# An fp32 cross-attention kernel on one core: product 6 of y by blocks from the second batch on, its state copied back into the bank, and two sums moved one period ahead

## The chip, the cores and the metric

The kernel runs on one core of a Trainium2 chip. Its time is device microseconds (us) of one execution; the median of 3 runs of the kernel before is 683.82 us (683.69 to 684.1). Beside these there is one profiled execution. The engines are called by their names in the profile: PE (TensorE, matmuls), PEld (its weight loads), DVE (VectorE), ACT (ScalarE), POOL (GpSimd) and SP (SyncE, which here only issues DMAs).

## The reference

Eight batches; x1 and x2 are 512 x 1024 each, all in fp32. Cut to what matters:

```python
q = einsum('bcn,dc->bnd', x1, Wq) + bq            # 1024 x 64
k = einsum('bcn,dc->bdn', x2, Wk) + bk            # 64 x 1024
v = einsum('bcn,dc->bdn', x2, Wv) + bv            # 512 x 1024
attn = softmax(einsum('bnd,bdm->bnm', q, k), axis=2)
out = einsum('bcm,bnm->bcn', v, attn) + x1
```

The kernel computes y = x2 times the unnormalised exponentials e, scales its columns by one over their sums, and then computes o = Wv y + bv + x1.

## The kernel before, in words

**Two products of matrices per batch, each in seven.** Both y and o are computed by the Winograd form of Strassen's method: with halves of rows, columns and depth, seven products (numbered 1 to 7, table MULT) of sums of quarters take the place of eight. For y the left operands are quarters of x2 transposed (`a["11"]` to `a["22"]`) and their sums S1 to S4, the right ones are quarters of e (`t["11"]` to `t["22"]`) and their sums T1 to T4. All operands lie in SBUF, [128, 4, 256] on the left and [128, 4, 512] on the right. The products accumulate in two pairs of PSUM banks, "a" and "c" (`a0`, `a1`, `c0`, `c1`), each bank [128, 512]: product 1 opens bank a, products 6 and 5 are added to it, so that after each of the three the bank holds a state (P1, P1+P6, P1+P6+P5) that some result needs. The states are taken out to SBUF as `s.tmp[1]`, `[6]` and `[5]`. The other four PSUM banks are two slots with the tag "sc".

**Plain and blocked products.** A plain product (`multiply`, line 374, matmuls at line 389) takes 8 matmuls of 512 columns (16 records in the trace, since an fp32 matmul shows as two). A blocked one uses the same seven-product scheme once more inside: 7 inner products (`inner_product`, line 452, matmuls at line 456) of 2 matmuls of 256 columns each, 28 records. Its order is fixed as inner products 1, 7, 6, 2, 5, 4, 3 and its operands are sums which DVE makes beforehand: `inner_left` (line 421) gives four steps of 256 columns in the order S3, S1, S2, S4, and `inner_right` (line 433) three steps, T1 and T3 in one of 1024 columns, then T2 and T4 of 512 each. Inner product 7 needs inner S3 and T3, inner product 6 needs inner S2 and T2, inner product 3 needs inner S4. `multiply_seeded` (line 473) starts from empty banks; inner results that have more than one destination go through an "sc" slot and an ACT copy. `multiply_onto` (line 503) adds to a bank that already holds something: what can go straight to the bank does, the rest is copied by ACT into an SBUF tile d; then `complete` (a DVE addition on d) and `join` (two DVE additions of bank and d, one for each row block) give the sum. The bank alone is then not the state.

**A period.** `period` (line 780) writes out one batch's order by hand; tc.manual_schedule keeps each engine to the order of the program. In batches 1 to 7 PE runs: products 1 and 2 of y (blocked), 6 (plain, `first(6)`), the four score tiles of the next batch's first half and, except in the last two batches, the queries of the batch after that, then products 5, 7 and 3 (blocked), scores of the second half, keys, product 4 (blocked), and the seven plain products of o (`second`). Batch 6 has no queries and no keys in between, batch 7 no scores either. DVE meanwhile makes the operands of the blocked products, takes results out of PSUM, folds maxima and sums (`folds`, `fold_halves`, lines 249 to 253), and subtracts the maximum (line 302). POOL reduces over the partitions (`highest`, line 268, and `total`, line 272, both PARTITION_ALL_REDUCE) and issues the accumulating DMAs. `weave` interleaves several lists, one step of each in turn.

**Around the change.** At the start of a late period the program has, for DVE: T1 and T2 (`sum_e`, line 315, four additions of 1024 columns), `complete` of product 1, the sum of half 1 folded (with the four `inner_left` steps of product 7 woven in), a reciprocal, `complete` of product 2, `evict_y` of 11, then the operands of product 5 and S4 (line 109), then the maxima of the next batch's scores. Just in front of it, at the end of the period before, DVE has the operands of products 1 and 2 of the new batch, then `fold_halves` of the sum of half 0 (which waits for an accumulating DMA of POOL, `add_tile`, line 636), then the two additions of `evict_o` 21.

Of the kernel before, what the change touches and what calls it, by code (L numbers as in the profile page):

```python
# [16 lines left out]
def kernel(  # L17
# [294 lines left out]
    def right_sums(t, k):  # L312

        x, y = {"T1": ("12", "11"), "T2": ("T1", "22"), "T3": ("22", "12"), "T4": ("21", "T2")}[k]
        nc.vector.tensor_tensor(t[k], t[x], t[y], ALU.add if k == "T4" else ALU.subtract)
# [8 lines left out]
    def sum_t4(s):  # L324

        s.t["T4"] = t4 = sb.tile([P, MH, H], F32, tag="eT4", name=f"eT4_{s.b}")
        if s.b == 0:
            sum_e(s, "T4")
            return
        for i in (0, 2):  # L330
            nc.scalar.copy(t4[:, i : i + 2, :], s.t["21"][:, i : i + 2, :])
        for i in (0, 2):
            nc.gpsimd.dma_start(t4[:, i : i + 2, :], s.t["T2"][:, i : i + 2, :], accum_op=ALU.add)

    def sum_t3(s, i):

# [3 lines left out]

    def copy_u1(s, j):
        if j == 0:
            s.tmp[1] = sb.tile([P, 2, H], F32, tag="yT1", name=f"uy1_{s.b}")
        nc.scalar.copy(s.tmp[1][:, j, :], s.bank["a", j])

    def sum_e(s, *ks):
        parts = [{n: v[:, i : i + 2, :] for n, v in s.t.items()} for i in (0, 2)]
        for k in ks:
            for part in parts:
                right_sums(part, k)  # L350

    def sum_y(s, k):
        y = s.y
# [149 lines left out]
    def multiply_onto(s, i, d_tag, v_tag, hooks={}):  # L503

        bank = MULT[i][2]
        b0, b1 = (s.bank[bank, j] for j in range(2))  # L510
        chain, third = inner_parts(s, i)
        d = sb.tile([P, 2, 2, H // 2], F32, tag=d_tag, name=f"d{i}_{s.b}", bufs=1 + (d_tag == "a21"))
        v = sb.tile([P, 2, H], F32, tag=v_tag, name=f"v{i}_{s.b}")[:, 0, left]
        steps = {
            1: (chain, True, d[:, 0, 0, :]),
            7: (third, True, v),
            6: (chain, False, d[:, 1, 0, :]),
            2: (b0[:, left], False),
            5: (chain, False, d[:, 0, 1, :], d[:, 1, 1, :]),
            4: (b1[:, left], False),  # L520
            3: (b0[:, right], False),
        }
        for z in (1, 7, 6, 2, 5, 4, 3):
            inner_product(s, i, z, *steps[z])
            if z in hooks:
                hooks[z]()

        def complete():
            both = v.unsqueeze(1).to_broadcast([P, 2, H // 2])
            nc.vector.tensor_tensor(d[:, 1], d[:, 1], both, ALU.add)  # L530

        return d.rearrange("p j a n -> p j (a n)"), complete
# [3 lines left out]
        d, complete = multiply_onto(s, 4, "u5" if s.b < B - 1 else "a21", "r", hooks)  # L536
        return [complete, lambda: nc.vector.tensor_tensor(s.tmp[6], s.tmp[6], d, ALU.add)]

    def multiply_5(s, hooks):

        s.tmp[5], complete = multiply_onto(s, 5, "u5", "r", hooks)
        complete()

        def join(j):
            d = s.tmp[5][:, j, :]
            nc.vector.tensor_tensor(d, s.bank["a", j], d, ALU.add)

        return [lambda: join(0), lambda: join(1)]

    def copy_7(s, j):  # L550
        if j == 0:
# [219 lines left out]
    def scores_and(n, h, i_bank, bank, project):  # L771

        for i in range(MH):
            scores(n, h, i, bank if i == i_bank else None)()
        return project()
# [4 lines left out]
    def period(s, n, nn, nnn):  # L780
# [3 lines left out]
        def first(i):  # L784
            multiply(s, "y", i, s.a, s.t, MH)
# [18 lines left out]

        def scores_0(*rows):
            then = scores_and(n, 0, 1, "c", next_queries if nn else nothing)
            weave(folds(n, 0, "max", ALU.max), *rows)
            highest(n, 0)
            return then
# [6 lines left out]
            copy_first(n, 0)  # L816
            add_tile(n, 0, 1)

        open_t(s)
        if n is None:  # L820
            load_x(s, x1)
        if s.b == 0:
            first(1)
            head_second(s, n)
            sum_e(s, "T1", "T2")
            fold_halves(s, 0, ALU.add)
            total(s, 0)
            load_a(n, "11")
            first(2)
            evict_y(s, "11")  # L830
            keys(n)
            load_x(nn, x1)
            sum_t4(s)
            sums(s, 1)
            shares(s, 0)
            sum_e(s, "T3")
            load_a(n, "21", "22")
            first(6)
            scores_0()
            weave(inner_left(s, 4, s.a["22"], "a12"), inner_right(s, 4, s.t["T4"], "eT2"))  # L840
            lefts_3 = inner_left(s, 3, s.a["S4"], "aI3")
            shares(s, 1)
            first(5)
            weave(lefts_3, inner_right(s, 3, s.t["22"], "eT1"))
            for i in range(MH):
                lower(n, 0, i)
            first(7)
            copy_7(s, 0)
            copy_7(s, 1)
            complete_3 = multiply_seeded(s, 3, "r")  # L850
            complete_3()
            evict_t3(s)
            evict_y(s, "22")
            scale_y(s, "T3", "11", "22")
        else:
            complete_1 = multiply_seeded(s, 1, "y11")
            sum_e(s, "T1", "T2")
            complete_1()
            if n:
                weave(folds(s, 1, "sum", ALU.add), inner_left(s, 7, s.a["S3"], "yT4"))  # L860
            else:
                weave(inner_left(s, 5, s.a["S1"], "i2"), inner_right(s, 5, s.t["T1"], "y21", "u1"))
                weave(folds(s, 1, "sum", ALU.add), inner_left(s, 7, s.a["S3"], "yT4"))
            total(s, 1)
            invert(s, 0)
            complete_2 = multiply_seeded(
                s, 2, "y22", {5: lambda: copy_u1(s, 0), 4: lambda: copy_u1(s, 1)}
            )
            if n:
                sum_t3(s, 0)  # L870
                sum_t3(s, 2)
            complete_2()
            evict_y(s, "11")
            if n is None:
                sum_e(s, "T3")
            sum_t4(s)
            first(6)
            if n:
                weave(
                    inner_left(s, 5, s.a["S1"], "i2"),  # L880
                    inner_right(s, 5, s.t["T1"], "y21", "u1"),
                    [lambda: sum_a(s, "S4")],
                )
            else:
                sum_a(s, "S4")
            evict_q = None
            if n:
                evict_q = scores_0()
            spread(s, 0)
            shares(s, 1)  # L890
            weave(inner_right(s, 7, s.t["T3"], "yT1", "yT2"), inner_left(s, 3, s.a["S4"], "aI3"))
            join_5 = multiply_5(s, {6: evict_q} if nn else {})
            weave(join_5, inner_right(s, 3, s.t["22"], "eT1"))
            if n:
                lower(n, 0, 0)
            complete_7 = multiply_seeded(s, 7, "y12")
            complete_7()
            evict_y(s, "22")
            if n:
                for i in range(1, MH):  # L900
                    lower(n, 0, i)
            else:
                weave(inner_left(s, 4, s.a["22"], "a12"), inner_right(s, 4, s.t["T4"], "eT2"))

            hooks = {2: lambda: copy_7(s, 0), 5: lambda: copy_7(s, 1)}
            if n:
                hooks |= {6: lambda: exponential(n, 0, 0), 4: lambda: exponential(n, 0, 1)}
            complete_3 = multiply_seeded(s, 3, "r", hooks)
            complete_3()
            evict_t3(s)  # L910
# [17 lines left out]
        tops = folds(n, 1, "max", ALU.max) if n else []  # L928
        if s.b == 0:
            value_sums("S1", "S2")  # L930
        if late and n:
            tops.pop(0)()
        sum_y(s, "T1")
        if s.b == 0:
# [7 lines left out]
            if nn is None:  # L942
                hooks[7] = first_sum
        join_4 = multiply_4(s, hooks)
        weave(join_4, tops[:2] if late else [])
        if late and n:
            negate(n, "S3")
        if n:
# [3 lines left out]
        evict_y(s, "21")  # L952
        lefts_1 = rights_2 = []
        if late and n:
            tops[2]()
            lefts_1 = inner_left(n, 1, n.a["11"], "i2")
            rights_2 = inner_right(n, 2, n.e[0][:, 1], "eT4")
        scale_y(s, "21")
# [1 line left out]
            step()  # L960
        sum_y(s, "T4")
        if late and n:
            highest(n, 1)
            add_11(n, "S3")
            weave(rights_2, lefts_1[1:])
# [32 lines left out]
        if n:  # L998
            rows = [inner_right(n, 1, n.e[0][:, 0], "yT1", "yT2"), inner_left(n, 2, n.a["12"], "aS4")]
            if s.b == 0:  # L1000
                rows += [inner_right(n, 2, n.e[0][:, 1], "eT4")]
            weave(*rows)
            second(3)
            evict_o(s, "12")
            second(4)
            fold_halves(n, 0, ALU.add)
            total(n, 0)
            evict_o(s, "21")
        else:
            second(4)  # L1010
            evict_o(s, "21")
            second(3)
            evict_o(s, "12")
# [37 lines left out]
```

## Time and profile before

| what | us |
|---|---|
| median of the runs shown | 683.82 |
| the profiled execution, its own time | 684.41 |
| its span in the trace | 682.6 |
| PE busy in the span | 672.3 (98%) |
| DVE busy | 602.6 (88%) |
| ACT busy | 337.7 (49%) |
| POOL busy | 224.5 (33%) |
| period of batches 1 to 5 | about 82.0 each |
| period of batch 6 | 78.85 |
| batch 7 to the end of the span | 73.03 |

A period is counted from the first matmul of its product 1 to that of the next (120.58, 202.58, 284.57, 366.56, 448.60, 530.72 and 609.57 us from the start of the span). In the timeline each line gives the start, the length, the engine, the line of the kernel, the operation, what it writes and reads, the number of instructions merged into the line, and in brackets the idle time of the engine just before with what ended it. An instruction's length overlaps the next one's start by some 0.07 us, so what a chain of DVE instructions takes is read from start to start.

### The profile page before, as it was taken

To read this page: it belongs to the slowest core of one execution; us is meant where nothing else is said; L and a number is where in the kernel's file an instruction comes from. 1 tells how busy PE (TensorE), PEld (TensorE's weight loads), DVE (VectorE), ACT (ScalarE), POOL (GpSimd) and SP (SyncE) were. 2 spreads that over 40 slices of the span, in tenths; PEclk is the share of its full clock that TensorE was granted. 3 is DMA by queue.
4 is the path that set the end of the run, shared out by engine and by line. 5 is a ranking of instruction groups with operands and counts; after the bars stand their busy time and mean duration, and the time that the engine had idled before them with its cause. 6 is when DMAs were issued, how large, how long until landed. Compare 5 with 4: busy or idle time off the path is not lost.

```text
span 682.6 us, 7284 instructions
## 1 busy us (share of the span) xinstructions
PE 672.3 (98%) x2444; PEld 402.4 (59%) x2444; DVE 602.6 (88%) x783; ACT 337.7 (49%) x570; POOL 224.5 (33%) x182
## 2 busy tenths in 40 slices
PE   9999999999999999999999999999999999899997
PEld 5333554757546665557646485474854767457753
DVE  1999898799999799889999899988999979969984
ACT  2744266366454464553744647535565446454320
POOL 0124215260454313542144421445025440452300
PEclk9999999999999999999999999999999999999999
DMA  9655758968896939959499694996969873489503
GB/s 301 269 192 210 184 204 149 244 126 249 240 248 168 252 101 296 224 155 267 110 293 234 151 267 110 269 227 142 255 121 223 212 167 49 92 155 270 132 12 111
DMA packets 50772, 131.09 MB, mean 192 GB/s; under 512 B 5552, under 2 KB 7856, under 8 KB 50736
## 3 DMA queue, kind: packets, MB, share of 16 engines
q0 software_dynamic: 22464, 54.60, 44.1%
q1 hardware_dynamic: 27984, 75.64, 30.8%
q10 hardware_dynamic: 288, 0.39, 0.2%
q8 instruction: 19, 0.31, 0.2%
q14 instruction: 17, 0.14, 0.1%
HBM read 87.30 MB, written 16.81 MB: 153 GB/s over the span
## 4 chain that ended last, share of the span: by engine, by line
PE 85%; DVE 7%; DMA 3%; issue 3%; ACT 1%; POOL 1%; SPq 0%; DVEq 0%; POOLq 0%; ACTq 0%
PE ps_oa L389 10%; PE ps_ya L389 9%; PE ps_ya L456 7%; PE ps_yc L456 7%; PE ps_oc L389 7%; PE ps_s L229 6%; PE ps_q L182 4%; PE ps_o L389 4%; PE ps_k L182 3%; PE ps_o L409 3%; PE ps_i4chain L456 3%; PE ps_i3chain L456 3%; PE ps_i5chain L456 2%; PE ps_i7chain L456 2%; PE ps_i1chain L456 2%
## 5 line engine op out<-in xcount | busy, mean ns | idle before, releaser
L272 POOL PARTITION_ALL_REDUCE den<-sum x16 | 52.6, 3285 | 94.2 <-DVE sum L253 94.2
L268 POOL PARTITION_ALL_REDUCE top<-max x16 | 44.5, 2779 | 103.4 <-DVE max L253 51.4
L302 DVE TENSOR_TENSOR e<-e,top 128x1024 f32<-128x1024 f32 x60 | 69.9, 1214 | 1.7 <-POOL top L268 1.7
L636 POOL DMA_DIRECT2D sum<-e x21 | 28.5, 1356 | 117.0 <-ACT sum L641 45.8
L306 ACT ACTIVATE e<-e 128x1024 f32<-128x1024 f32 x60 | 61.8, 1056 | 4.4 <-DVE e L302 3.8
L389 PE MATMUL ps_ya<-eT,aS 128*128 128x512 f32 x144 | 63.5, 594 | 0.0
L389 PE MATMUL ps_oa<-yT,w_S 128*128 128x512 f32 x128 | 57.5, 592 | 0.0
L389 PE MATMUL ps_oc<-yT,w 128*128 128x512 f32 x128 | 57.4, 592 | 0.0
L238 ACT COPY e<-ps_s 128x1024 f32<-128x1024 f32 x46 | 45.6, 1030 | 8.8 <-PE ps_s L229 8.8
L229 PE MATMUL ps_s<-q,k 64*128 64x512 f32 x188 | 47.9, 608 | 0.9 <-ACT q L662 0.8
L389 PEld LDWEIGHTS ps_ya<-eT,aS 128*128 128x128 f32 x144 | 27.2, 190 | 32.1 <-issue 29.5
L389 PEld LDWEIGHTS ps_oa<-yT,w_S 128*128 128x128 f32 x128 | 24.3, 190 | 30.6 <-issue 30.6
L389 PEld LDWEIGHTS ps_oc<-yT,w 128*128 128x128 f32 x128 | 24.3, 190 | 30.6 <-issue 30.4
L249 DVE TENSOR_TENSOR max<-max,e 128x1024 f32<-128x1024 f32 x30 | 36.7, 1222 | 1.8
L400 ACT COPY uo<-ps_oa 128x512 f32<-128x512 f32 x32 | 18.6, 586 | 36.1 <-PE ps_oa L389 31.5
L229 PEld LDWEIGHTS ps_s<-q,k 64*128 64x128 f32 x188 | 17.0, 186 | 24.7 <-issue 17.7
L493 ACT COPY ps_ya<-ps_i1chain 128x256 f32<-128x256 f32 x28 | 10.0, 357 | 42.2 <-PE ps_i1chain L456 38.7
L389 PE MATMUL ps_o<-y,w 128*128 128x512 f32 x64 | 29.0, 595 | 1.9 <-DVE y L563 1.8
L249 DVE TENSOR_TENSOR max<-e 128x1024 f32<-128x1024 f32 x15 | 18.3, 1220 | 12.4 <-ACT e L236 12.3
L389 PE MATMUL ps_oa<-y,w_S 128*128 128x512 f32 (+1 forms) x68 | 28.8, 567 | 0.0
L409 PE MATMUL ps_o<-y,w 128*128 128x512 f32 x64 | 28.8, 592 | 0.0
L563 DVE TENSOR_TENSOR y<-y,den 128x1024 f32<-128x1024 f32 x24 | 28.6, 1219 | 0.1
(202 smaller groups left out, 1566.3 us busy)
## 6 DMA issues: line engine op xcount, KB each, us to landing
x_in_x_dram<-in_x_dram SPq DMA_DIRECT2D x60, 512.0 KB, 7.0
a<-in_x2T_dram SPq DMA_DIRECT2D x32, 512.0 KB, 9.2
sum<-e POOLq DMA_DIRECT2D x21, 512.0 KB, 9.3
aS<-in_x2T_dram POOLq DMA_DIRECT2D x14, 512.0 KB, 8.5
uo<-in_x_dram POOLq DMA_DIRECT2D x14, 512.0 KB, 10.1
r<-in_x_dram POOLq DMA_DIRECT2D x14, 512.0 KB, 11.2
out_dram<-r SPq DMA_DIRECT2D x14, 512.0 KB, 4.8
eT<-eT POOLq DMA_DIRECT2D x14, 512.0 KB, 10.4
```

Of the source, the lines that this page charges most:

```text
L182: nc.tensor.matmul(ps[r, :], w_sb[:, c, :], s.x[:, c, ts(h, H)], start=(c == 0), stop=(c == CT - 1),)
L229: nc.tensor.matmul(ps[g], s.k[r, ts(i, P)], s.q[r, ts(h, H)], start=True, stop=True)
L238: nc.scalar.copy(e[:, :, i, :], whole)
L249: nc.vector.tensor_tensor(f, e[:, :, 0, :] if i == 1 else f, e[:, :, i, :], op)
L268: nc.gpsimd.partition_all_reduce(s.top[h], s.mx[h][:, 0, :], P, ReduceOp.max)
L272: nc.gpsimd.partition_all_reduce(s.den[h], s.mx[h][:, 0, :], P, ReduceOp.add)
L302: nc.vector.tensor_tensor(e, e, top, ALU.subtract)
L306: nc.scalar.activation(e, e, AF.Exp)
L389: nc.tensor.matmul(ps[:, n], left[ka][:, k, ts(j, P)], right[kb][:, k, n], start=opens and k == 0, stop=i in (2, 3, 4) and k == n_k - 1, s ...
L409: nc.tensor.matmul(ps, w["11"][:, k, ts(j, P)], s.y["11"][:, k, :], start=k == 0, stop=False, skip_group_check=True)
L456: nc.tensor.matmul(ps, s.inner[i][ka][:, k, :], s.inner[i, "t"][kb][:, k, :], start=opens and k == 0, stop=z in (2, 3, 4) and k == MH // 2 ...
L563: nc.vector.tensor_tensor(s.y[k], s.y[k], rden, ALU.mult)
```

## The change

From batch 1 on, product 6 of y becomes a blocked product on top of bank a. Its operands are made on DVE during products 1 and 2; its result is completed and joined with the bank by DVE, and ACT writes the joined state P1+P6 back into bank a (`reseed`), since product 5 is added on it; where there are score tiles, `reseed` stands in `scores_0` behind their copies. T1 and T2 of the next batch move from the start of its period to the end of the period in front: three of the four additions go ahead of `fold_halves` and `evict_o` 21, the fourth behind them. The operands of product 7's left side move from products 1 and 2 to product 6, product 5's left side from product 6 to the score folds (in the last batch, both sides of product 5 move from product 1 to product 6). The copies for T3 and T4 on ACT are put at fixed inner products of products 2 and 6. In batch 6 the folding of the second half's maxima moves from around product 4 to behind the last sum of y.

```diff
-        for i in (0, 2):
-            nc.scalar.copy(t4[:, i : i + 2, :], s.t["21"][:, i : i + 2, :])
-        for i in (0, 2):
-            nc.gpsimd.dma_start(t4[:, i : i + 2, :], s.t["T2"][:, i : i + 2, :], accum_op=ALU.add)
+    def copy_t4(s, i):
+        t4 = s.t["T4"][:, i : i + 2, :]
+        nc.scalar.copy(t4, s.t["21"][:, i : i + 2, :])
+        nc.gpsimd.dma_start(t4, s.t["T2"][:, i : i + 2, :], accum_op=ALU.add)
...
+    def multiply_joined(s, i, v_tag, hooks={}):
+        s.tmp[i], complete = multiply_onto(s, i, f"u{i}", v_tag, hooks)
         def join(j):
-            d = s.tmp[5][:, j, :]
+            d = s.tmp[i][:, j, :]
             nc.vector.tensor_tensor(d, s.bank["a", j], d, ALU.add)
+        return [complete, lambda: join(0), lambda: join(1)]
+    def reseed(s):
+        for j in range(2):
+            nc.scalar.copy(s.bank["a", j], s.tmp[6][:, j, :])
...
             complete_1 = multiply_seeded(s, 1, "y11")
-            sum_e(s, "T1", "T2")
-            complete_1()
-            if n:
-                weave(folds(s, 1, "sum", ALU.add), inner_left(s, 7, s.a["S3"], "yT4"))
-            else:
-                weave(inner_left(s, 5, s.a["S1"], "i2"), inner_right(s, 5, s.t["T1"], "y21", "u1"))
-                weave(folds(s, 1, "sum", ALU.add), inner_left(s, 7, s.a["S3"], "yT4"))
+            weave(
+                folds(s, 1, "sum", ALU.add),
+                [nothing, complete_1] + inner_right(s, 6, s.t["T2"], "yT1", "yT2"),
+                [nothing, nothing] + inner_left(s, 6, s.a["S2"], "i2"),
+            )
             total(s, 1)
             invert(s, 0)
...
             complete_2()
             evict_y(s, "11")
             sum_t4(s)
-            first(6)
+            hooks = {6: lambda: copy_t4(s, 0), 5: lambda: copy_t4(s, 2)}
+            complete_6, *join_6 = multiply_joined(s, 6, "v", hooks)
             if n:
                 weave(
-                    inner_left(s, 5, s.a["S1"], "i2"),
                     inner_right(s, 5, s.t["T1"], "y21", "u1"),
-                    [lambda: sum_a(s, "S4")],
+                    inner_left(s, 7, s.a["S3"], "yT4"),
+                    [nothing, lambda: sum_a(s, "S4")],
                 )
+                complete_6()
+                weave(join_6)
+                evict_q = scores_0(inner_left(s, 5, s.a["S1"], "i2"))
+                rights_7 = inner_right(s, 7, s.t["T3"], "yT1", "yT2")
             else:
+                weave(
+                    inner_left(s, 5, s.a["S1"], "a11"),
+                    inner_right(s, 5, s.t["T1"], "y21", "u1"),
+                    inner_left(s, 7, s.a["S3"], "yT4"),
+                )
+                complete_6()
+                weave(join_6)
+                reseed(s)
+                sum_e(s, "T3")
+                rights_7 = inner_right(s, 7, s.t["T3"], "yT1", "yT2")
+                rights_7.pop(0)()
                 sum_a(s, "S4")
...
-        if late and n:
+        if late and nn:
             tops.pop(0)()
...
-        weave(join_4, tops[:2] if late else [])
+        weave(join_4, tops[:2] if late and nn else [])
...
         sum_y(s, "T4")
         if late and n:
+            if nn is None:
+                weave(tops, lefts_1[1:])
+                lefts_1 = []
             highest(n, 1)
...
             second(4)
+            open_t(n)
+            *early, last = sums_e(n, "T1", "T2")
+            weave(early)
             fold_halves(n, 0, ALU.add)
             total(n, 0)
             evict_o(s, "21")
+            last()
```

More of the change, by code (lines that the diff above doesn't have):

```diff
@@ L328, in sum_t4 @@
             sum_e(s, "T4")
-            return
-        for i in (0, 2):
-            nc.scalar.copy(t4[:, i : i + 2, :], s.t["21"][:, i : i + 2, :])
-        for i in (0, 2):
-            nc.gpsimd.dma_start(t4[:, i : i + 2, :], s.t["T2"][:, i : i + 2, :], accum_op=ALU.add)
+    def copy_t4(s, i):
+        t4 = s.t["T4"][:, i : i + 2, :]
+        nc.scalar.copy(t4, s.t["21"][:, i : i + 2, :])
+        nc.gpsimd.dma_start(t4, s.t["T2"][:, i : i + 2, :], accum_op=ALU.add)
     def sum_t3(s, i):
@@ L342, in copy_u1, with sums_e @@
         if j == 0:
-            s.tmp[1] = sb.tile([P, 2, H], F32, tag="yT1", name=f"uy1_{s.b}")
+            s.tmp[1] = sb.tile([P, 2, H], F32, tag="y21", name=f"uy1_{s.b}")
         nc.scalar.copy(s.tmp[1][:, j, :], s.bank["a", j])
+    def sums_e(s, *ks):
+        parts = [{n: v[:, i : i + 2, :] for n, v in s.t.items()} for i in (0, 2)]
+        return [lambda k=k, part=part: right_sums(part, k) for k in ks for part in parts]
     def sum_e(s, *ks):
[L347 to L350, printed above, removed]
+        weave(sums_e(s, *ks))
     def sum_y(s, k):
@@ L512, in multiply_onto @@
         d = sb.tile([P, 2, 2, H // 2], F32, tag=d_tag, name=f"d{i}_{s.b}", bufs=1 + (d_tag == "a21"))
-        v = sb.tile([P, 2, H], F32, tag=v_tag, name=f"v{i}_{s.b}")[:, 0, left]
+        if v_tag == "v":
+            v = sb.tile([P, H // 2], F32, tag="v", name=f"v{i}_{s.b}")
+        else:
+            v = sb.tile([P, 2, H], F32, tag=v_tag, name=f"v{i}_{s.b}")[:, 0, left]
         steps = {
@@ L537, in multiply_4 @@
         return [complete, lambda: nc.vector.tensor_tensor(s.tmp[6], s.tmp[6], d, ALU.add)]
-    def multiply_5(s, hooks):
-        s.tmp[5], complete = multiply_onto(s, 5, "u5", "r", hooks)
-        complete()
+    def multiply_joined(s, i, v_tag, hooks={}):
+        s.tmp[i], complete = multiply_onto(s, i, f"u{i}", v_tag, hooks)
         def join(j):
-            d = s.tmp[5][:, j, :]
+            d = s.tmp[i][:, j, :]
             nc.vector.tensor_tensor(d, s.bank["a", j], d, ALU.add)
-        return [lambda: join(0), lambda: join(1)]
+        return [complete, lambda: join(0), lambda: join(1)]
+    def reseed(s):
+        for j in range(2):
+            nc.scalar.copy(s.bank["a", j], s.tmp[6][:, j, :])
     def copy_7(s, j):
@@ L806, in scores_0 @@
             then = scores_and(n, 0, 1, "c", next_queries if nn else nothing)
+            if late:
+                reseed(s)
             weave(folds(n, 0, "max", ALU.max), *rows)
@@ L817, in first_sum @@
             add_tile(n, 0, 1)
-        open_t(s)
         if n is None:
@@ L822, in period @@
         if s.b == 0:
+            open_t(s)
             first(1)
@@ L864, in period @@
             total(s, 1)
             invert(s, 0)
-            complete_2 = multiply_seeded(
-                s, 2, "y22", {5: lambda: copy_u1(s, 0), 4: lambda: copy_u1(s, 1)}
-            )
+            hooks = {5: lambda: copy_u1(s, 0), 4: lambda: copy_u1(s, 1)}
             if n:
-                sum_t3(s, 0)
-                sum_t3(s, 2)
+                hooks |= {6: lambda: sum_t3(s, 0), 3: lambda: sum_t3(s, 2)}
+            complete_2 = multiply_seeded(s, 2, "y22", hooks)
             complete_2()
@@ L873, in period @@
             evict_y(s, "11")
-            if n is None:
-                sum_e(s, "T3")
             sum_t4(s)
-            first(6)
+            hooks = {6: lambda: copy_t4(s, 0), 5: lambda: copy_t4(s, 2)}
+            complete_6, *join_6 = multiply_joined(s, 6, "v", hooks)
+            evict_q = None
             if n:
                 weave(
-                    inner_left(s, 5, s.a["S1"], "i2"),
                     inner_right(s, 5, s.t["T1"], "y21", "u1"),
-                    [lambda: sum_a(s, "S4")],
-                )
-            else:
+                    inner_left(s, 7, s.a["S3"], "yT4"),
+                    [nothing, lambda: sum_a(s, "S4")],
+                )
+                complete_6()
+                weave(join_6)
+                evict_q = scores_0(inner_left(s, 5, s.a["S1"], "i2"))
+                rights_7 = inner_right(s, 7, s.t["T3"], "yT1", "yT2")
+            else:
+                weave(
[5 more added lines that the diff above has]
+                weave(join_6)
+                reseed(s)
+                sum_e(s, "T3")
+                rights_7 = inner_right(s, 7, s.t["T3"], "yT1", "yT2")
+                rights_7.pop(0)()
@@ L885, in period @@
                 sum_a(s, "S4")
-            evict_q = None
-            if n:
-                evict_q = scores_0()
             spread(s, 0)
             shares(s, 1)
-            weave(inner_right(s, 7, s.t["T3"], "yT1", "yT2"), inner_left(s, 3, s.a["S4"], "aI3"))
-            join_5 = multiply_5(s, {6: evict_q} if nn else {})
+            weave(rights_7, inner_left(s, 3, s.a["S4"], "aI3"))
+            complete_5, *join_5 = multiply_joined(s, 5, "r", {6: evict_q} if nn else {})
+            complete_5()
@@ L954, in period @@
         if late and n:
-            tops[2]()
+            if nn:
+                tops[2]()
             lefts_1 = inner_left(n, 1, n.a["11"], "i2")
```

## The prediction

> **What bounds the kernel now.** First the page's busy shares: PE is busy 98% of the span and DVE 88%. The waits of PE itself (the view of waits for PE alone) come to some 6 us in the whole span, so in most batches PE has no gap: a batch lasts as long as its matmuls, and only fewer matmuls, or a new wait of PE, can move the end. DVE is the engine next to it.
>
> ```profile
> PE 672.3 (98%) x2444; PEld 402.4 (59%) x2444; DVE 602.6 (88%) x783; ACT 337.7 (49%) x570; POOL 224.5 (33%) x182
> ```
>
> Next the timeline of PE in batch 3 (period from 284.57). Product 2 has its 7 inner products 0.863 us apart (6.04 in all); product 6 runs from 296.65 to 303.62.
>
> ```profile
> 290.61 1.03 PE L456 MATMUL ps_i2chain<-e,a 128*128 128x256 f32 x4
> ...
> 295.79 1.03 PE L456 MATMUL ps_yc<-e,aI 128*128 128x256 f32 x4
> 296.65 7.03 PE L389 MATMUL ps_ya<-eT,aS 128*128 128x512 f32 x16
> 303.62 1.13 PE L229 MATMUL ps_s<-q,k 64*128 64x512 f32 x4
> ```
>
> Then the timeline of DVE around that period's start, with T1 (two additions), T2 (two), and the wait for POOL's accumulating DMA in front:
>
> ```profile
> 284.70 0.69 DVE L253 TENSOR_TENSOR sum<-sum 128x512 f32<-128x512 f32 x1 [2.18 <-DMA sum<-e]
> 285.31 1.41 DVE L628 SCALAR_TENSOR_TENSOR o<-ps_oc,bv_sb,uo 128x512 f32<-128x512 f32 x2
> 286.63 3.31 DVE L315 TENSOR_TENSOR eT<-e,e 128x1024 f32<-128x1024 f32 x2
> 289.87 2.35 DVE L315 TENSOR_TENSOR eT<-eT,e 128x1024 f32<-128x1024 f32 x2
> ```
>
> T1 takes 3.24 where T2, of the same size, takes 2.27. The reason is in the next view, POOL and DVE after the maxima of batch 3:
>
> ```profile
> 346.89 0.68 DVE L253 TENSOR_TENSOR max<-max 128x512 f32<-128x512 f32 x1
> 347.49 1.22 DVE L563 TENSOR_TENSOR y<-y,den 128x1024 f32<-128x1024 f32 x1
> 348.63 1.26 DVE L429 TENSOR_TENSOR aI<-a 128x256 f32<-128x256 f32 x1
> ```
> ```profile
> 347.68 2.68 POOL L268 PARTITION_ALL_REDUCE top<-max  x1 [3.05 <-DVE max L253]
> ```
>
> The 256-column addition takes 1.26 against 0.41 to 0.42 elsewhere. A DVE addition of two SBUF operands that starts about 1 us into POOL's all-reduce is **held**. For the sums' all-reduce the next free start lies 2.89 us after the start of `fold_halves` (284.70 to 287.59: T1's first addition began at 286.63 and the second one 2.10 later, against 1.14 normally, so 0.97 held). Additions with a PSUM operand run through it (evict_y in product 2's end).
>
> **What PE gains.** Product 6 has 6.97 us from its start to the scores' and 6.86 where no change of shape follows (batch 7, 621.66 to 628.52). Blocked it takes 6.04, as each blocked product does. That is 0.82 less, in seven batches 5.7 us, if no operand is late.
>
> **What DVE gets.** Start to start, 1024 columns take 1.14, 512 take 0.60, 256 take 0.34. Per batch: right side 1.14 + 2 x 0.60 = 2.34, left side 4 x 0.34 = 1.36, complete 0.60, joins 2 x 0.60: 5.5 us. Batch 3 has waits of DVE of 2.18, 1.90, 0.33, 0.68, 0.78, 0.48 and 0.39 = 6.7 us, so the sum fits; the question is when each operand is ready. The moves: T1 and half of T2 go into the 2.18 wait (DVE is free 2.04 before the period's start; three additions, 3.42, end at +1.38). The 1.90 wait, for the scores' copies, takes the joins.
>
> **The chain to product 6.** Inner product 6 of product 6 is due two products and two inner products into the period, 12.08 + 1.73 = **+13.81**, and needs inner S2, the third left step. Count from X, the start of `fold_halves` of half 0. It takes 0.60, evict_o 21 takes 1.32, T2's last addition would start at X + 1.92, just where T1 started before, is held to X + 2.89 and ends at X + 4.03. Then three folds and the first right step (4 x 1.14), complete of product 1 (0.60), S3 (0.34), fold_halves of half 1 (0.60), T2 (0.60), S1 (0.34), T4 (0.60), S2 (0.41): X + 12.08, and 0.14 until PE starts (as from 636.67 to 636.81 in batch 7): X + 12.22 without a second hold. But half 1's fold_halves releases the second all-reduce. Before, PSUM work ran during it and 0.19 was lost; now T4 and S2, two SBUF operands each, start 1.54 and 2.14 behind that fold. If T4 is held to 2.89, S2 is 1.35 late; if POOL gets in only behind T4, some 0.9. No row shows a start at 1.54 (the nearest that was held is at 1.73), so the ends are 0 and 1.35 and I take 1.14: **X + 13.36**.
>
> *Batches 2 to 5*: X = +1.38 (the DMA landed at -1.0 to +1.35 there), ready at +14.76, a wait of 0.95, less 0.82: +0.13 each, **+0.5**. *Batch 1*: the DMA lands at 124.70, X = +4.12, ready at +17.48: a wait of 3.67, less 0.82: **+2.85**.
>
> Product 5's inner product 6 has a second such date: DVE ends S4 of product 6 and the reciprocal at +14.95; complete 2 and evict_y 1.8; product 5's right side, product 7's left side and S4 4.84; complete 6 and joins 1.8; three folds with three left steps 4.65 with PE's delay: +28.05. In batches 2 to 5 queries lie between (3.6 us) and it is due at 28.1, covered.
>
> *Batch 6* has no queries: product 5 would end 32.37 instead of 29.45, **+2.9**. Its later moved folds take 4.0 us of DVE from in front of the scaling of y 21, for which PE waited 1.81 (591.03 to 592.30): some 2.0 back. Net **+0.9**.
>
> *Batch 7*: the three T additions end at +1.7, the DMA at about +2.4, X = 2.4. Product 6 ends at 15.76 + 5 x 0.863 = 20.08 (before 18.95). DVE: 15.98 + 1.8 + 5.06 (11 operand steps) + complete and join 0 = 24.05; `reseed`'s first copy 0.57 and two handovers: 24.95. Product 5's inner product 2 writes the bank and is due at 22.67: **a wait of 2.3 us in the place of none**. Product 5 ends at 28.4 (before 25.0). The 1.22 wait in product 7 (for its right side, line 445) goes: T2 of product 7 is ready at 30.1, due at 30.13. With that, product 3 starts 1.9 late; the 0.3 wait before o's product 2 shrinks: **+1.6**.
>
> What is costed at nothing: `reseed` in batches 1 to 6 (0.57 a copy by line 413, PSUM to PSUM; the bounds are this and 1.05, an SBUF copy twice as long) ends near +25 and the bank is written at +29; without that cover it would be batch 7's 2.3. ACT's other 1.6 us lie in its 38 idle us a batch. T4's copies go some 2 us later, their DMAs land 10.4 later near +30, used at +46. T3's DMAs, queued on POOL behind the second all-reduce and the reciprocal, go no later than now; its readers move 2 back. fold_halves and the first all-reduce go 1.2 later with evict_o 21 (out's DMA on SP with them): bank c is needed at +7.1 and free at +3.3, the reciprocal is read at +15.
>
> Sum: 2.85 + 0.5 + 0.9 + 1.6 = 5.85; 684.41 + 5.85 = 690.3. The median lies 0.6 under the profiled time: **689.7**.
>
> [...]
>
> **Rivals.** *The second hold does not come.* For it: in batch 6 the all-reduce at 591.22 let DVE run through and took 7.50 itself. Against it: all the others held the addition that came in their way. Then S2 is ready at +13.6 in batches 2 to 5 and PE has its 0.82 four times: -3.3; batches 1, 6 and 7 are 1.14 better each (+1.7, -0.2, +0.5): -1.3, or 682.5. If T2's last addition isn't held either (0.97), batches 1, 6 and 7 give +0.7, -1.2 and -0.5: -4.2, 679.6. This is the case on the faster side; it decides at a hold of 0.2 us, the margin between 13.6 and 13.81. *DVE becomes the bound.* Its list is 82.0 - 6.7 + 5.5 + 0.95 = 81.8 against 82.1 for the batch with its new wait; for it speak the 0.3 us left, against it that its waits for PE (0.48 and 0.39) vanish when it is late. Each further 0.5 us that it loses (a longer hold, S1 held too, 0.34) costs 0.5 in seven batches: 693 to 696. *The operands are never late* (all 5.7 us and batch 6's 2.0: 676) is spoken against by batch 1's DMA at 124.70.
>
> **Numbers.** The forecast's own range is 686.5 to 692.5, chance 0.65; no second hold or none, 679 to 683.5, 0.25; DVE the bound, 0.10. Leaving out the ends: 681.5 to 693. A measurement of this kernel can tell about 0.2%, 1.4 us, from no change: faster by that 0.18, within 0.10, slower 0.72.
>
> **What would show it.** Right: PE waits in front of inner product 6 of product 6 (weights `aI` or `eI6`) by DVE, longest in batch 1, some 1 us in batches 2 to 5; in batch 7 PE waits in product 5 for ACT's copy into ps_ya; T4 of product 6 (line 449) or S2 lasts over 1 us; batches 2 to 5 stay near 82.1. Wrong: periods of 81.2 there, or PE waits at another product.

## The result and the profile after

The changed kernel takes **708.41 us** (median of 4 runs, 707.89 to 709.43) beside 683.96 of the kernel before on the same chip (683.69 to 684.46): a ratio of 1.0358 (95% interval 1.0341 to 1.0376), slower by 24.5 us. The forecast was 689.7, the whole of its range 681.5 to 693. The profiled execution after has 707.89 of its own and a span of 706.1, against 684.41 and 682.6.

First the head of the page after: the busy times by engine, then the row of the clock that PE was granted, in 40 slices of 17.65 us.

```profile
PE 675.8 (96%) x2528; PEld 423.8 (60%) x2528; DVE 656.3 (93%) x853; ACT 348.5 (49%) x605; POOL 221.9 (31%) x182
...
PEclk9999999899999999999999999998999999999999
```

PE was to have 5.7 us less to do, and yet its busy time has grown by 3.5 us. The two 8s (slices 8 and 28, in batches 1 and 5) say why: there it ran part of the time at a lower clock. The mean clock fell from 1.000 to 0.985. Next the view of waits for PE alone (who waited, for whom, us in total, how often, the longest):

```profile
PE ps_i6chain L458 <- DVE aI L431: 16.7, 7, 3.4
PE ps_i5chain L458 <- ACT d L467: 2.1, 1, 2.1
PE ps_i5chain L458 <- DVE aI L431: 1.8, 1, 1.8
```

Inner product 6 of product 6 waits in each of the seven batches, as the prediction said, but for 16.7 us in all; 16.7 / 7 = 2.4 on average. The periods, from product 1 to the next product 1, in us (batch 5 of the kernel before starts at 448.72; the 448.60 in the list of starts further up is a slip):

| batch | 1 | 2 | 3 | 4 | 5 | 6 | 7 |
|---|---|---|---|---|---|---|---|
| before | 81.99 | 81.99 | 81.99 | 82.16 | 81.99 | 78.86 | 73.03 |
| after | 88.07 | 83.21 | 83.22 | 83.22 | 87.52 | 80.41 | 80.76 |
| difference | +6.1 | +1.2 | +1.2 | +1.1 | +5.5 | +1.55 | +7.7 |
| predicted | +2.85 | +0.13 | +0.13 | +0.13 | +0.13 | +0.9 | +1.6 |

These come to +24.4; the start of batch 1 came 0.9 earlier (119.68 against 120.58; over the ten kernels of this study it lies between these two, and the cause was not sought), which leaves the span's 23.5. There are two kinds of batch: a steady loss of 1.2, and jumps in batches 1, 5 and 7.

**A steady batch.** The timeline of PE in batch 3 (period from 290.97), where product 6 was one line of 7.03 before:

```profile
303.92 1.03 PE L458 MATMUL ps_i6third<-eI6yT,aI 128*128 128x256 f32 x4
306.62 1.10 PE L458 MATMUL ps_i6chain<-eI6yT,aI 128*128 128x256 f32 x4 [1.67 <-DVE aI L431]
```

These are inner products 7 and 6 of product 6. They start 2.70 apart in the place of 0.863, so the second is 1.84 late, which eats the 0.82 saved and 1.0 more. The timeline of DVE in the same batch, with T1 and half of T2 now first and the left steps of product 6 (line 431) at the end:

```profile
288.84 2.35 DVE L315 TENSOR_TENSOR eT<-e,e 128x1024 f32<-128x1024 f32 x2
...
292.25 0.69 DVE L253 TENSOR_TENSOR sum<-sum 128x512 f32<-128x512 f32 x1
...
294.17 2.18 DVE L315 TENSOR_TENSOR eT<-eT,e 128x1024 f32<-128x1024 f32 x1
...
301.87 0.68 DVE L253 TENSOR_TENSOR sum<-sum 128x512 f32<-128x512 f32 x1
...
303.07 2.46 DVE L431 TENSOR_TENSOR aI<-aS 128x256 f32<-128x256 f32 x1
305.46 0.68 DVE L451 TENSOR_TENSOR eI6yT<-eT,eI6yT 128x512 f32<-128x512 f32 x1
306.06 0.87 DVE L431 TENSOR_TENSOR aI<-aS,aI 128x256 f32<-128x256 f32 x2
```

And POOL beside it:

```profile
293.04 3.23 POOL L272 PARTITION_ALL_REDUCE den<-sum  x1 [3.14 <-DVE sum L253]
...
302.66 3.59 POOL L272 PARTITION_ALL_REDUCE den<-sum  x1 [5.49 <-DVE sum L253]
```

T1 has lost its hold (2.35 where it took 3.31) and T2's last addition has it (2.18, start to next start 2.10 against 1.13), both as predicted. The second hold falls on S1: 256 columns, 2.39 from start to start where 0.34 is normal, so **2.05 lost**. It starts 1.20 after `fold_halves`, where the prediction let it pass; T4 behind it (305.46, 0.60 to the next start) is free. S1 lasts 2.46 or 2.47 in all seven batches.

**A batch with a jump.** The timeline of PE in batch 1 after:

```profile
138.13 2.04 PE L458 MATMUL ps_i6chain<-eI6yT,aI 128*128 128x256 f32 x4 [3.42 <-DVE aI L431]
139.97 1.91 PE L458 MATMUL ps_ya<-eT,aS 128*128 128x256 f32 x4
141.68 1.48 PE L458 MATMUL ps_i6chain<-eI6yT,aI 128*128 128x256 f32 x4
142.99 1.03 PE L458 MATMUL ps_ya<-eI6yT,aS 128*128 128x256 f32 x4
```

Behind the wait the starts lie 1.84, 1.71 and 1.31 apart, not 0.863: 4.86 - 3 x 0.863 = 2.27 us are lost after the operand has come. The view by windows gives the clock there: the columns are the window, its length, each engine's busy time and instructions, the granted clock, the DMA share and GB/s. The rows are the stretches behind the waits of batches 1 (3.42), 3 (1.67), 5 (3.18) and 7 (the second one, 2.06, which came 8 us behind one of 3.42).

```profile
138.13:142.99 4.86, 4.86 (x12) 3.92 (x13) 4.83 (x10) 1.32 (x2) 3.65 (x5) 0.54 0.49 85
306.62:311.00 4.38, 4.38 (x20) 3.68 (x20) 4.35 (x9) 2.83 (x5) 3.70 (x5) 1.00 0.47 81
474.56:481.02 6.46, 6.46 (x16) 5.22 (x17) 6.42 (x12) 2.28 (x5) 3.67 (x5) 0.54 0.66 119
...
653.84:658.22 4.38, 4.38 (x12) 3.52 (x13) 4.35 (x7) 0.59 (x2) 0.36 (x1) 0.61 0.32 80
```

A wait of 1.67 left the clock at 1.00; behind the others it was 0.54 to 0.61 over 4 to 6 us (0.61 behind the 3.42 of batch 7 too). These are means of a window: in batch 1 the clock is 0.50 from 135.8 to 142.5 and 1.00 from 142.65 on. Taking from each slow stretch 0.863 per inner product gives 2.27 in batch 1, 6.46 - 4 x 0.863 = 3.01 in batch 5, 1.76 and 1.79 in batch 7: **8.8 us in all**, for which the prediction has no term.

**Batch 7.** The timeline of PE, and then that of ACT, where product 5 waits for the reseeded bank:

```profile
650.75 1.03 PE L458 MATMUL ps_i5third<-eI5y,aI 128*128 128x256 f32 x4
653.84 1.39 PE L458 MATMUL ps_i5chain<-eI5u,aI 128*128 128x256 f32 x4 [2.06 <-ACT d L467]
```
```profile
652.30 1.19 ACT L557 COPY ps_ya<-d 128x512 f32<-128x512 f32 x2 [2.34 <-DVE d L550]
653.42 0.37 ACT L467 COPY d<-ps_i5chain 128x256 f32<-128x256 f32 x1
```

Inner product 6 of product 5 needs the slot that ACT empties into d, and on ACT this copy stands behind both copies of `reseed`. So the wait comes one inner product earlier than predicted and includes the second copy.

### The profile page after: what moved, and what is told of

Same layout as the page of the kernel before. It is cut to its first block, busy times and chain, and to the rows that moved or that the text cites. A ratio compares the mean times of both kernels' runs of the same rounds, so it can differ in the third digit from the quotient of the medians.

```text
span 706.1 us, 7562 instructions
## 1 busy us (share of the span) xinstructions
PE 675.8 (96%) x2528; PEld 423.8 (60%) x2528; DVE 656.3 (93%) x853; ACT 348.5 (49%) x605; POOL 221.9 (31%) x182
## 4 chain that ended last, share of the span: by engine, by line
PE 57%; DVE 26%; DMA 8%; issue 5%; POOL 2%; ACT 1%; SPq 1%; DVEq 0%; POOLq 0%; ACTq 0%
PE ps_ya L458 8%; PE ps_oa L391 6%; PE ps_yc L458 5%; DMA sum<-e 5%; DVE aI L431 4%; PE ps_s L229 4%; DVE eT L315 4%; DVE sum L249 4%; PE ps_q L182 3%; PE ps_i3chain L458 3%; PE ps_oc L391 3%; PE ps_o L411 3%; PE ps_i5chain L458 3%; PE ps_i4chain L458 3%; PE ps_i7chain L458 3%
## 5 line engine op out<-in xcount | busy, mean ns | idle before, releaser
L272 POOL PARTITION_ALL_REDUCE den<-sum x16 | 55.1, 3446 | 80.1 <-DVE sum L253 75.2
L268 POOL PARTITION_ALL_REDUCE top<-max x16 | 39.2, 2450 | 122.6 <-DVE max L253 104.1
L645 POOL DMA_DIRECT2D sum<-e x21 | 28.5, 1356 | 122.0 <-ACT sum L650 51.5
L458 PE MATMUL ps_i6chain<-eI6yT,aI 128*128 128x256 f32 x56 | 19.0, 473 | 16.7 <-DVE aI L431 16.7
L431 DVE TENSOR_TENSOR aI<-aS 128x256 f32<-128x256 f32 x44 | 32.6, 741 | 0.0
L229 PEld LDWEIGHTS ps_s<-q,k 64*128 64x128 f32 x188 | 16.7, 186 | 22.2 <-issue 15.4
L431 DVE TENSOR_TENSOR aI<-a 128x256 f32<-128x256 f32 x58 | 27.5, 476 | 0.0
```

Of the source, the lines that this page charges most:

```text
L229: nc.tensor.matmul(ps[g], s.k[r, ts(i, P)], s.q[r, ts(h, H)], start=True, stop=True)
L268: nc.gpsimd.partition_all_reduce(s.top[h], s.mx[h][:, 0, :], P, ReduceOp.max)
L272: nc.gpsimd.partition_all_reduce(s.den[h], s.mx[h][:, 0, :], P, ReduceOp.add)
L431: return lambda: nc.vector.tensor_tensor(v[k], v[x], v[y], op)
L458: nc.tensor.matmul(ps, s.inner[i][ka][:, k, :], s.inner[i, "t"][kb][:, k, :], start=opens and k == 0, stop=z in (2, 3, 4) and k == MH // 2 ...
```

## The experiments

The theory after these traces has three parts: (A) S1 is held by the second all-reduce of the sums; (B) a wait of PE of over 3 us (3.42 and 3.18 here) is followed by some us at half clock (0.50 from 135.8 to 142.5 in batch 1); (C) batch 7 pays in addition for `reseed`. The rival to A is that DVE's list is simply full; the rival to B is that the slow matmuls come from something else in these batches. The 95% intervals stand behind the ratios, and all ratios are to the kernel before.

**The fold of half 1 behind the operands.** The all-reduce then runs beside additions that read PSUM.

```diff
+            *fold_1, halves_1 = folds(s, 1, "sum", ALU.add)
             weave(
-                folds(s, 1, "sum", ALU.add),
+                fold_1,
                 [nothing, complete_1] + inner_right(s, 6, s.t["T2"], "yT1", "yT2"),
                 [nothing, nothing] + inner_left(s, 6, s.a["S2"], "i2"),
             )
+            halves_1()
             total(s, 1)
```

> The changed kernel, but half 1's fold_halves (and with it POOL's all-reduce) stands behind the operand steps of product 6 on DVE, so that the all-reduce runs beside additions that read PSUM. Theory A (the all-reduce holds step S1 of product 6's left side for some 2 us, PE then waits for S2, and after a wait of over 3 us runs at a lower granted clock for some microseconds): S1 takes its usual 0.4 us, PE's wait before inner product 6 of product 6 goes to 0 in batches 2 to 4 and to under 2.5 in batches 1 and 7, the granted clock stays at 1.00 there; 683 to 690 us. Rival B (DVE simply has too much to do, 93% of the span, wherever the steps stand): 702 to 708.

Measured: 693.62, ratio 1.0145 (1.0129 to 1.016). Its timeline of DVE in batch 3 (S1, then the first PSUM addition behind the fold, then product 5's first right step), and that of POOL:

```profile
297.28 0.42 DVE L431 TENSOR_TENSOR aI<-aS 128x256 f32<-128x256 f32 x1
...
299.71 0.67 DVE L501 TENSOR_TENSOR ps_yc<-ps_yc,v 128x512 f32<-128x512 f32 x1
...
301.60 1.52 DVE L447 TENSOR_TENSOR eI5y<-eT 128x1024 f32<-128x1024 f32 x1
```
```profile
299.81 3.22 POOL L272 PARTITION_ALL_REDUCE den<-sum  x1 [7.82 <-DVE few L280]
```

S1 takes 0.42, the PSUM additions run through the all-reduce at their usual lengths (0.67, and two in 1.27, as in the changed kernel behind its all-reduce, at 306.94 and 307.52), and only 0.30 is lost on the next two-SBUF addition. Batches 2 to 4 fall to 81.47 (before: 81.99), with the same list for DVE: for the steady batches A holds and the full list is refuted. The time itself lies outside both expectations (683 to 690 and 702 to 708): the kernel stays 10 us slower, with 84.29 in batch 1, 80.24 in batch 6 and 80.16 in batch 7. In batch 7 PE, now nearly on time in product 6 (waits of 0.88 and 0.77), waits 4.77 in product 5 for the copy into d, and the clock falls there (the next starts lie 1.86, 1.71 and 1.71 apart, not 0.863; mean clock of the run 0.993); in batch 6 it falls in product 5, at the end of a wait of only 1.84:

```profile
558.80 2.04 PE L458 MATMUL ps_i5chain<-eI5u,aI 128*128 128x256 f32 x4 [1.84 <-DVE aI L431]
```

**No second all-reduce.** This tells the hold apart from the order of DVE, which stays that of the change.

```diff
+        if s.b and h == 1:
+            nc.gpsimd.memset(s.den[h], 1.0)
+        else:
+            nc.gpsimd.partition_all_reduce(s.den[h], s.mx[h][:, 0, :], P, ReduceOp.add)
```

> The changed kernel in its own order, but POOL fills half 1's sums with ones by a memset in place of the all-reduce (batches 1 to 7): the sum over the partitions of half 1 is left out. DVE's list is the same. Theory A (the hold by the all-reduce): S1 takes 0.4 us, the wait before inner product 6 shrinks by about 2 in every batch, 686 to 694 us. Rival B (DVE has too much to do): 704 to 708.

Measured: 689.66, 1.0088 (1.0072 to 1.0105). Batches 2 to 4 have 81.17, which is 0.82 under before: the whole predicted gain of PE. The hold and what it brings with it is worth 708.41 - 689.66 = 18.8 us. What is left above before lies in batch 1 (83.87, +1.9) and batch 7 (79.82, +6.8). Its waits of PE:

```profile
PE ps_i5chain L461 <- ACT d L470: 3.7, 1, 3.7
PE ps_i6chain L461 <- DVE aI L434: 3.5, 3, 1.4
```

That this median is the predicted number is chance: it has no hold and a batch 7 that costs four times what was predicted.

**Each part of the change alone.** Only T1 and T2 moved, put into the kernel before (the first diff); and the change with T1 and T2 back at the start of the period (the second).

```diff
-            sum_e(s, "T1", "T2")
             complete_1()
...
             second(4)
+            open_t(n)
+            parts = [{k: v[:, i : i + 2, :] for k, v in n.t.items()} for i in (0, 2)]
+            early = [(k, part) for k in ("T1", "T2") for part in parts]
+            for k, part in early[:3]:
+                right_sums(part, k)
             fold_halves(n, 0, ALU.add)
             total(n, 0)
             evict_o(s, "21")
+            right_sums(early[3][1], "T2")
```
```diff
+            open_t(s)
             complete_1 = multiply_seeded(s, 1, "y11")
+            sum_e(s, "T1", "T2")
...
             second(4)
-            open_t(n)
-            *early, last = sums_e(n, "T1", "T2")
-            weave(early)
             fold_halves(n, 0, ALU.add)
             total(n, 0)
             evict_o(s, "21")
-            last()
```

> The kernel before with T1 and T2 made at the end of the period in front, product 6 plain. Theory A: the move alone puts three additions into a wait of DVE and costs nothing that PE waits for: 683 to 685 us. Rival C (the move delays fold_halves, the all-reduce and evict_o 21 so that somebody waits): over 686.

Measured: 682.50 over 10 runs, 0.9982 (0.9973 to 0.9992). This is 0.5 under the range expected. Periods 1 to 6 stay as before, and batch 7 goes from 73.03 to 71.27: the move is worth nothing where no operand of the plain product 6 was late, and in batch 7 the wait of 1.2 in product 7 is gone.

> The changed kernel with T1 and T2 back at the start of the period, product 6 blocked. Theory A: DVE starts the operands of product 6 some 3 us later, so PE waits some 4 us or more in every batch, and the granted clock falls in every batch: 725 to 745 us. Rival C (the move is what costs): under 705.

Measured: 729.77, 1.066 (1.0611 to 1.0709). In its profiled execution (723.33, mean clock 0.979) the periods of batches 1 to 5 are 85 to 91, and the waits of product 6 for DVE come to 26.8 in the place of 16.7 + 1.7 = 18.4, and product 2 waits 3.6 for ACT. So the blocked product needs the move, and the parts are not additive: +46.1 and -1.2 alone, +24.5 together.

The clock did not fall in every batch, as Theory A had it. In batches 2, 3 and 4 PE waits the same 3.42 in product 6. Behind the wait of batch 3 the clock stays at 1.00; the period is 85.27, and that of batch 2 is 85.40. Behind the wait of batch 4 the window has 0.65, and the period is 87.16. The timeline of PE in batches 3 and 4, then the windows behind these two waits:

```profile
313.50 1.10 PE L458 MATMUL ps_i6chain<-eI6yT,aI 128*128 128x256 f32 x4 [3.42 <-DVE aI L431]
...
399.11 1.10 PE L458 MATMUL ps_i6chain<-eI6yT,aI 128*128 128x256 f32 x4 [3.42 <-DVE aI L431]
```
```profile
313.50:318.00 4.50, 4.50 (x22) 3.71 (x22) 4.47 (x9) 2.91 (x5) 3.71 (x5) 1.00 0.50 87
399.11:404.00 4.89, 4.89 (x15) 3.99 (x16) 4.86 (x10) 1.95 (x5) 3.71 (x5) 0.65 0.54 95
```

So (B) is too simple: the length of the wait alone does not settle whether the clock falls. The last section sets the waits side by side.

**The gap filled with matmuls.** To tell B from its rival: three matmuls whose result nobody reads, into the unused half of an "sc" slot, between inner products 7 and 6 of product 6 in batches 1, 5 and 7.

```diff
+    def fill(s, count):
+        for _ in range(count):
+            nc.tensor.matmul(
+                s.spare, s.a["11"][:, 0, 0:P], s.t["11"][:, 0, :], start=True, stop=True, skip_group_check=True
+            )
...
+            if s.b in (1, 5, 7):
+                hooks[7] = lambda: fill(s, 3)
```

> The changed kernel with three extra matmuls of 512 columns into an unused half of a PSUM slot, between inner products 7 and 6 of product 6, in batches 1, 5 and 7 only (the ones with a wait of over 3 us); the operands come when they did. Theory A (the granted clock falls because PE stood still for over 3 us): the matmuls behind the wait run at full speed, 2 us or more are saved in each of the three, 700 to 703 us. Rival D (the matmuls there are slow for another reason, such as what DVE and ACT do at that time): 707 to 710.

Measured: 703.97, 1.0298 (1.028 to 1.0315). The timeline of PE in batch 1, then the window behind the gap:

```profile
135.32 2.84 PE L558 MATMUL ps_i6third<-e,a 128*128 128x512 f32 x6 [0.46 <-ACT v L467]
138.18 1.13 PE L458 MATMUL ps_i6chain<-eI6yT,aI 128*128 128x256 f32 x4
139.15 1.03 PE L458 MATMUL ps_ya<-eT,aS 128*128 128x256 f32 x4
```
```profile
138.18:142.70 4.52, 4.52 (x21) 3.72 (x21) 4.49 (x9) 2.91 (x5) 3.75 (x5) 1.00 0.41 71
```

Inner product 6 starts where it did (138.18 against 138.13), the clock stays at 1.00, and batch 1 gets 2.14 shorter (85.93), batch 5 3.05 (84.47). These are the 2.27 and 3.01 counted above from the starts, so the slow matmuls come from the standstill and rival D is refuted. Batch 7 gains only 0.14 (80.62): PE runs through product 6 at its usual pace and then waits 3.81 in product 5 where it waited 2.06, and the clock falls behind that wait (0.61 from 648.72 to 653.10). This is why the time is just above the 700 to 703 expected:

```profile
648.72 1.84 PE L458 MATMUL ps_i5chain<-eI5u,aI 128*128 128x256 f32 x4 [3.81 <-ACT d L467]
```

**No reseed.** Both calls of `reseed` are left out.

> The changed kernel without ScalarE's copies of the state back into bank a (the state after product 6 is left out of product 5's bank). Theory A (the copies are waited for in batch 7 alone): batch 7 loses its wait of 2.1 us in product 5 and what the clock takes there, 703 to 706 us; batches 1 to 5 stay as they are. Rival E (the copies delay ACT, and with it PE, in every batch): under 702.

Measured: 704.72, 1.0298 (1.028 to 1.0317). Batch 7 gives 78.25 (-2.5): the wait for d is gone, and the inner products of product 5 are 0.86 to 0.97 apart. Batches 1 to 4 and 6 stay within 0.7 of the change (batch 1: 88.74). Batch 5 has 85.93 in the place of 87.52: its wait in product 6 is 2.84 for 3.18, and the slow stretch behind it loses 1.8 for 3.0; why the wait is shorter there is not settled. So `reseed` costs nothing where scores follow, as predicted, and 2.5 in batch 7.

**Only where there is room.** T1 and T2 moved everywhere; product 6 blocked in batches 2 to 4 alone, with the fold of half 1 behind the operands and product 5's left steps one place ahead of the score folds; then the same in batches 2 to 5. The rest is as in the kernel before.

```diff
+    BLOCKED = (2, 3, 4)
...
-            if late:
+            if s.b in BLOCKED:
                 reseed(s)
-            weave(folds(n, 0, "max", ALU.max), *rows)
+            weave(*rows, folds(n, 0, "max", ALU.max))
...
+            if s.b in BLOCKED:
+                complete_1 = multiply_seeded(s, 1, "y11")
+                *fold_1, halves_1 = folds(s, 1, "sum", ALU.add)
...
+                complete_6, *join_6 = multiply_joined(s, 6, "v", hooks)
```

> A version that should beat both: T1 and T2 moved as in the change, product 6 blocked in batches 2 to 4 only, with half 1's fold_halves behind its operand steps and the left steps of product 5 one place ahead of the score folds; batches 1, 5, 6 and 7 as before the change. Theory A: three batches of about 81.2 in the place of 82.0, on top of the move's gain: 680.0 us (679.3 to 680.8). Rival B (DVE has too much to do): over 682.

Measured: **679.33** (679.08 to 680.23), 0.9938 (0.9924 to 0.9952): under both kernels, with batches 2 to 4 at 81.17, batch 7 at 71.13 and a mean clock of 1.000. In its waits of PE the only one of a product of y is the 0.5 of product 5 in the last line; the first is o's old wait for the scaling of y:

```profile
PE ps_o L398 <- DVE y L579: 1.8, 1, 1.8
...
PE ps_i5chain L465 <- ACT e L239: 0.5, 1, 0.5
```

> The same with product 6 blocked in batch 5 too. Theory A: batch 5 starts with DVE 1.5 us later than the others, so its S2 is late by up to 1 us: between 0.8 better and 0.5 worse than with batches 2 to 4, 679 to 681 us. Rival B: over 682.

Measured: 680.20 (679.72 to 680.76), 0.9947 (0.9934 to 0.996). Batch 5 has 82.02, as before, where batches 2 to 4 have 81.17: it brings nothing there.

## Why the prediction was wrong

The side was right (slower, 0.72), the wait and its place too; the size was 17.7 us short (23.5 in the span against 5.85). Two of its steps failed, the second hold and the clock. By its steps:

- **PE gains 0.82 per product 6**: right, shown by the runs without the hold (81.17).
- **DVE's 5.5 us fit into its waits**: right in batches 2 to 4, where the same list runs at 81.17 to 81.47. "DVE becomes the bound" was wrong as a rival, although its 693 to 696 lay nearest.
- **Which addition the second all-reduce holds: the step that failed.** I let S1 pass at 1.20 behind `fold_halves`, since no row had a start that early, and took T4 as held, S2 1.14 late. S1 was held, 2.05 long. "S1 held too" stood in the text as a further 0.34, but S1, held first, was held for 2.05, not for its own length. S2 ended at X + 14.22 (306.47, with X = 292.25) and not + 13.36. Those 0.9 us in seven batches are some 6 (an estimate from batch 3).
- **X in batches 5 and 7**: 2.79 and 4.1 for the 1.38 and 2.4 predicted: 3.1 us together. In batch 7 the accumulating DMA stands on POOL behind the maxima's all-reduce, which in batch 6 ended 9.8 before the period's start (before: 10.85), because its folds were moved. For batch 5 the cause lies in batch 4. There POOL could start the all-reduce of the maxima only behind the issue of a DMA that had waited 10.62 for ACT, and it took 5.25 where it takes 2.68 in batches 1 to 3, 5 and 6 (5.28 in batch 4 of the run with the fold last, too):

```profile
440.02 1.19 POOL L645 DMA_DIRECT2D sum<-e  x1 [10.62 <-ACT uo L402]
440.77 5.25 POOL L268 PARTITION_ALL_REDUCE top<-max  x1
```
```profile
446.05 4.63 DVE L302 TENSOR_TENSOR e<-e,top 128x1024 f32<-128x1024 f32 x4 [1.68 <-POOL top L268]
```

  DVE's additions ran on, and then it waited for the maxima. No run of its own was made on that; why only batch 4 stays open.
- **The clock: the other step that failed, and the largest miss**: 8.8 us for a term put at nothing. The prediction itself had a wait of 3.67 in batch 1 and priced it at 3.67; it asked of no wait what the matmuls behind it would cost.
- **Batch 7, "a wait of 2.3 us in the place of none"**: the wait is there (2.06), but its date is 28.5 into the period for the 24.95 predicted: X 1.7, the hold 0.9, and 1.0 since the copy of d stands on ACT behind both copies of `reseed`. PE came later as well, which hid most of that.
- **`reseed` at nothing in batches 1 to 6**: right. In batch 6 PE waits 0.83 in product 5 for a copy of `reseed` (line 557), but without the copies it waits the same 0.83 there for DVE, and the period is 80.40 for 80.41.
- **Batch 6**: +0.9 predicted, +1.55 measured.
- **The rival without a second hold**, 682.5, would have been wrong too: the run that has none gives 689.7, mostly through batch 7.

The misses add up: 8.8 (clock) + 6 (hold) + 3.1 (X) - 0.9 (start) = 17.0 of 17.7. The hold and the clock are shown by runs; the part of X rests on the traces alone. One sum of the prediction is off by 0.02 (1.38 + 13.36 is 14.74, not 14.76), which changes nothing.

## What to carry over

Where an operand has a due date, look up what runs on POOL at that moment: here the addition of two SBUF operands that met the all-reduce of the sums lost 2.05 where it came early and 0.30 where it came late, and additions that read PSUM in its place lost nothing (0.67, and two in 1.27, as without it). A wait of PE can cost more than its length: in the changed kernel 1.8 to 3.0 us more behind each of four waits of 2.06 to 3.42, although one of 3.42 in the run with T1 and T2 back was followed by a clock of 1.00. A change that has room in some batches should be made in those alone: with half 1's fold behind the operands, product 6 blocked in seven batches took 693.62 us, in three of them 679.33.

## What the runs showed of the hardware

- **The held additions got through before the recorded end of the all-reduce, for the sums by 1.13 us three times.** These are estimates: the start of the next instruction less the usual time of the held one. T2's last addition (all-reduce 293.04 to 296.27) got through as if started at 296.27 - 1.13 = 295.14, S1 (302.66 to 306.25) at 305.46 - 0.34 = 305.12, again 1.13 before the end, and line 447 with the fold last (299.81 to 303.03) at 301.60 + 0.30 = 301.90, once more 1.13. For the maxima in the kernel before (347.68 to 350.36) it was some 0.9, since the addition at 348.63 got through as if started at 349.47. S1 started 0.41 after the recorded start and was already held.
- **In batch 4 the all-reduce was long in place of DVE**: it took 5.25 for 2.68, while DVE's additions beside it (440.94 to 444.37) kept their usual 1.22, 0.42 and 0.68.
- **The clock fell behind some waits of PE and not behind others of the same length.** In the changed kernel it was 0.54 to 0.61 behind the waits of 3.42 (batches 1 and 7), 3.18 (batch 5) and 2.06 (batch 7, 8 us behind one of 3.42). It was 0.61 behind the 3.81 with the gap filled. Behind the 4.77 with the fold last and the 2.84 without `reseed` the starts lay up to 1.86 and 1.71 apart, for 0.863. With T1 and T2 back, the windows behind two waits of 3.42 have 1.00 (batch 3) and 0.65 (batch 4). A wait of 1.84 in product 5 of batch 6 left it at 1.00 in the changed kernel (574.16 to 578.56), but in the run with the fold last the matmuls behind the same wait of 1.84 took 2.04 where they take 1.10 in the changed kernel. The starts 1.84 and 1.71 apart behind the wait of batch 1 fit the 0.50 granted there (2 x 0.863 = 1.73).
- **How long it stayed low in the changed kernel**: from 135.75 to 142.58 and from 473.67 to 480.50, 6.83 us each, and from 644.34 to 647.75 and from 654.58 to 657.99, 3.41 us each. The first two falls came while PE still waited (it went on at 138.13 and 474.56), the last two behind the waits' ends (643.81 and 653.84). What decides between waits of the same length no run shows.
